# Seven block products for xn^T kn in a fused attention and feed-forward kernel

## Chip, cores and metric

The kernel runs on one core of one Trainium2 chip. The metric is the device time of one execution in microseconds. All data are float32.

## What is computed

The reference takes x of 8 batches by 1024 rows by 256 columns, normalises each row, and adds three things: x itself, a linear attention with 16 heads of 16 columns, and a feed-forward network of width 1024. Cut to what matters:

```python
xn = layernorm(x)
q, k, v = split(xn @ qkv_w + qkv_b)          # 16 heads of 16 columns each
q, k = l2norm(q), l2norm(k)
kv = einsum('bhnd,bhne->bhde', k, v)          # no softmax
attn = einsum('bhnd,bhde->bhne', q, kv) @ proj_w + proj_b
ffn = relu(xn @ W1 + b1) @ W2 + b2
out = x + attn + ffn
```

Since there is no softmax, the kernel does not compute v. It forms G = xn^T kn for each batch (a 256 by 256 matrix, summed over the 1024 rows; kn is the normalised k), then kv from G and the weights of v, and then M = kv proj_w, so that attention ends as one more product, q M, in the accumulation of the second feed-forward product.

## The kernel before, in words

Work goes batch by batch. A batch has 8 row tiles of 128 rows (NT is 8, HT is 4 tiles, a half of the rows); the 256 columns are KC, 2, halves of 128. The order of all instructions is written out by hand: each engine executes its own in the order in which the code issues them, and the framework adds the waits. Tiles come from pools by tag, and most tags ("turn", "u1", "u3", "gT", "xn", "x") have one buffer, so the next tile of a tag waits until all readers of the last one are done.

The loop over b at L822 to L858 has these stages:

- `hidden(b)` (L543) computes the first feed-forward product of batch b. It is already done by Strassen's scheme: a product of 2 by 2 blocks is formed from seven block products of sums of blocks instead of eight. Between its steps stand small steps: `mix_kv` and `mix_m` for M, the scaling and turning of q, and sums of blocks on GpSimd (`sums_of_h`, `sums_of_x`, `sums_of_q`; `sums_of_a` at L188 has the four subtractions and additions at L190, L191, L192 and L194).
- `project_by_sums(b + 1)` (L382) computes q and k of the next batch, by seven products too. It ends with the norms of k: reductions (L377), a maximum, a square root on ScalarE and a reciprocal on VectorE (L352 to L354), while GpSimd adds a bias (L442) and scales k by its norms, half by half (L466).
- `second(b)` (L683) is the second feed-forward product with q M joined to it, by seven products: banks a, c, d and e, of ten matmul records each. After four of them it yields. On VectorE stand u2 and u3 (L702), then, from `between`, `norms_of_q(b + 1)` (four squares on ScalarE at L376, four reductions at L377, L352 to L354), then the joining of bank e (L719) and a 32 by 32 transpose (L710), after which GpSimd adds to x (L715).
- Then come the layer norm statistics of batch b + 2 (`norm_stats` and `norm_scale`: eight statistics at L247, eight aggregations at L249, a root on ScalarE at L251, two small operations at L257 and L260).
- Then `mix_g(b + 1)` (L497): G as 16 matmuls, for each half of the columns of xn eight row tiles, 128 by 128 stationary with 256 columns of kn moving (L502), into one PSUM bank, and one copy to gT on ScalarE (L507).
- Then `norm_apply` (L271) and `turn_x` (L297) of batch b + 2, and the rest of `second(b)`: three more products, their joins, the stores. `shift(b + 2)` ends the round.

An fp32 matmul stands in the profile as two records, each with a weight load of its own, so the 16 matmuls of G are 32 records. The code around the change is this:

Of the kernel before, what the change touches and what calls it, by code (L numbers as in the profile page):

```python
# [9 lines left out]
F32 = mybir.dt.float32  # L10
AF = mybir.ActivationFunctionType
ALU = mybir.AluOpType
# [4 lines left out]
def kernel(  # L17
# [34 lines left out]
    nc = tc.nc  # L52
    P = 128
    B, N, C = x.shape
# [3 lines left out]
    NT = N // P  # L58
    HT = NT // 2
    HN = N // 2  # L60
    KC = C // P
# [11 lines left out]
    one = ctx.enter_context(tc.tile_pool(name="one", bufs=1))  # L73
# [3 lines left out]
    ps_mix = ctx.enter_context(tc.tile_pool(name="ps_mix", bufs=1, space=bass.MemoryType.PSUM))  # L77
# [12 lines left out]
    def bank(shape, name):  # L90

        return psum.tile(shape, F32, tag="bank", name=name)

    xs, xqs, xns, xnTs, xSs, hTs, qks, qTs, mixes, Ms, hSs = ({} for _ in range(11))
# [13 lines left out]
    def load_squares(b, halves=(0, 1)):  # L108
        xqs[b] = one.tile([P, 2, R, HT, CJ], F32, tag="xq", name=f"xq_{b}")
        for n in halves:  # L110
            for j in range(R):
                nc.sync.dma_start(out=xqs[b][ts(j, S), n], in_=squares_v(x, b, n, j))
# [75 lines left out]
    def sums_of_a(eng, blocks, s1, s2, s4, s3=True):  # L188
        a11, a12, a21, a22 = blocks
        eng.tensor_tensor(s1, a21, a22, ALU.add)  # L190
        eng.tensor_tensor(s2, s1, a11, ALU.subtract)  # L191
        eng.tensor_tensor(s4, a12, s2, ALU.subtract)  # L192
        if s3:
            eng.tensor_tensor(a21, a11, a21, ALU.subtract)  # L194
# [46 lines left out]
    def norm_stats(b, tiles):  # L241

        xt, n = xs[b], len(tiles)
        st = work.tile([P, NT, 6], F32, tag="st", name=f"st_{b}_{tiles[0]}")[:, :n, :]
        mv = small.tile([P, NT, 2], F32, tag="mv", name=f"mv_{b}_{tiles[0]}")[:, :n, :]
        for i, t in enumerate(tiles):
            nc.vector.bn_stats(st[:, i, :], xt[:, t, :])  # L247
        for i in range(n):
            nc.vector.bn_aggr(mv[:, i, :], st[:, i, :])  # L249
        rstd = small.tile([P, NT], F32, tag="rstd", name=f"rstd_{b}_{tiles[0]}")[:, :n]  # L250
        nc.scalar.activation(rstd, mv[:, :, 1], AF.Sqrt, bias=eps_sb)  # L251
        for i, t in enumerate(tiles):
            stats[b, t] = i, mv, rstd

    def norm_scale(b, tiles, on_act):
        i, mv, rstd = stats[b, tiles[0]]
        nc.vector.reciprocal(rstd, rstd)  # L257
        if on_act:
            nmr = small.tile([P, NT], F32, tag="nmr", name=f"nmr_{b}_{i}")[:, : len(tiles)]
            nc.vector.scalar_tensor_tensor(nmr, mv[:, :, 0], -1.0, rstd, ALU.mult, ALU.mult)  # L260
            for t in tiles:
                stats[b, t] += (nmr,)
# [87 lines left out]
    def invert(ss):  # L350

        nc.vector.tensor_scalar_max(ss, ss, L2_EPS * L2_EPS)  # L352
        nc.scalar.activation(ss, ss, AF.Sqrt)
        nc.vector.reciprocal(ss, ss)  # L354
# [19 lines left out]
    def squares_of(b, n, g, m, ss):  # L374
        sq = work.tile([P, 2, C], F32, tag="yt", name=f"sq_{b}_{n}_{g}_{m}")
        nc.scalar.activation(sq, part_of_qk(b, n, g, m), AF.Square)  # L376
        return lambda: nc.vector.tensor_reduce(  # L377
            ss[:, n * HT + 2 * g : n * HT + 2 * g + 2, :],
            sq.rearrange("p w (g d) -> p w g d", d=D), AX.X, ALU.add,
        )  # L380
# [69 lines left out]
    def norms_of_q(b):  # L450
        ss = small.tile([P, NT, H], F32, tag="ssq", name=f"ssq_{b}", bufs=1)
        late = []
        for n in range(2):
            for g in range(2):
                late.append(squares_of(b, n, g, 0, ss))
                if len(late) == 2:
                    late.pop(0)()
        late.pop(0)()
        invert(ss)
        for h in range(2):  # L460
            norms_of[b, h, 0] = ss[:, ts(h, HT), :]
# [35 lines left out]
    def mix_g(b):  # L497
        qk, xn = qks[b], xns[b]
        gp = ps_mix.tile([P, KC, C], F32, tag="mix", name=f"gp_{b}")
        for f in range(KC):  # L500
            for t in range(NT):
                nc.tensor.matmul(  # L502
                    gp[:, f, :], xn[:, t, ts(f, P)], qk[:, t, C : 2 * C],
                    start=(t == 0), stop=(t == NT - 1),
                )
        gT = one.tile([P, KC, C], F32, tag="gT", name=f"gT_{b}")
        nc.scalar.copy(gT, gp)  # L507
        mixes[b] = gT

    def mix_kv(b):  # L510
        gT = mixes.pop(b)
        kvp = ps_mix.tile([P, KC, P], F32, tag="mix", name=f"kvp_{b}")
        for c in range(KC):
            cols = slice(2 * C + c * P, 2 * C + (c + 1) * P)
            for f in range(KC):
                nc.tensor.matmul(  # L516
                    kvp[:, c, :], wqkv_sb[:, f, cols], gT[:, f, ts(c, P)],
                    start=(f == 0), stop=(f == KC - 1),
                )
        kvm = one.tile([P, KC, P], F32, tag="Mt", name=f"kvm_{b}")  # L520
        for c in range(KC):
            nc.vector.tensor_tensor(
                kvm[:, c, :].rearrange("p (g d) -> p g d", d=D),
                kvp[:, c, :].rearrange("p (g d) -> p g d", d=D),
                blk.unsqueeze(2).to_broadcast([P, G, D]), ALU.mult,
            )
        mixes[b] = kvm
# [141 lines left out]
    def sums_of_q(b):  # L669
        sums_of_a(  # L670
            nc.vector if b == B - 1 else nc.gpsimd,
            halves(qTs[b]), *(hSs[b][:, s, FH] for s in range(3)),
        )

    def product(dst, lhs, rhs, start, stop):

        for n, (l, r) in enumerate(zip(lhs, rhs)):
            nc.tensor.matmul(  # L678
                dst, l, r, start=start and n == 0, stop=stop and n == len(lhs) - 1,
                skip_group_check=True,  # L680
            )

    def second(b, between=lambda: None):  # L683

        xq, hT, hS, qT, (M, Mt) = xqs[b], hTs[b], hSs[b], qTs[b], Ms[b]
        a11, a12, s3, a22 = (
            [hT[:, i + k * FH, ts(n, HP), :, :] for i in range(FH)] + [qT[:, k, ts(n, HP), :, :]]
            for n in range(2) for k in range(2)
        )
        s1, s2, s4 = ([hS[:, s, i] for i in range(FH + 1)] for s in range(3))  # L690
        b11, t3, b21, b22 = (
            [w2_sb[:, i + k * FH, ts(m, HC)] for i in range(FH)] + [M[:, k, ts(m, HC)]]
            for k in range(2) for m in range(2)
        )
        t1, t2, t4 = ([w2t[:, s, i, :] for i in range(FH)] + [Mt[:, s, :]] for s in range(3))

        def tmp(name):
            pool = work if name in ("u2", "yt") else one
            return pool.tile([P, HP, P, 2], F32, tag=name, name=f"{name}_o_{b}")

        def add(dst, p, q):
            nc.vector.tensor_tensor(dst, p, q, ALU.add)  # L702
            return dst
# [37 lines left out]
        a, c_, d, e = (bank([P, HP, P, 2], f"po{s}_{b}") for s in "acde")  # L741
# [4 lines left out]
        u1 = tmp("u1")  # L746
        nc.scalar.copy(u1, a)
        product(c_, t2, s2, True, True)
        u2 = add(tmp("u2"), c_, u1)
        u3 = tmp("u3")  # L750
        for du, u in zip(ds, parts):
            product(du, t3, [r[:, u] for r in s3], True, False)
# [69 lines left out]
    for b in range(B):  # L822
        if b > 0:
            load_squares(b, (0,) if b == B - 1 else (0, 1))
            if b + 2 < B:
                load(b + 2)
        hidden(b)
        if b == 0:
            qTs[0] = one.tile([P, KC, NP, P, 2], F32, tag="qT", name="qT_0")
            turn_on_pe(qTs[0], qks[0], "q_0")  # L830
            sums_of_w2()
            sums_of_q(0)
            shift(1)
        if b + 1 == 1:
            project(1)
            out_parts = second(b)
        elif b + 1 < B:
            project_by_sums(b + 1)
            out_parts = second(b, lambda: norms_of_q(b + 1))
        else:  # L840
            out_parts = second(b)
        next(out_parts)
        if b + 1 == 1:
            sums_of_x(1, 0)
            sums_of_x(1, 1)
            sums_of_wqk()
        if b + 2 < B:
            norm_stats(b + 2, range(NT))
            norm_scale(b + 2, range(NT), True)
        if b + 1 < B:  # L850
            mix_g(b + 1)
        if b + 2 < B:
            norm_apply(b + 2, range(NT))
            for _ in range(R):
                turn_x(b + 2)
        next(out_parts)
        if b + 2 < B:
            shift(b + 2)  # L858
# [31 lines left out]
```

## Time and profile before

| what | value |
|---|---|
| median of 3 runs | 625.96 us (624.41 to 626.52) |
| the profiled execution's own time | 624.22 us |
| its span, first to last instruction | 622.1 us |
| mean granted TensorE clock | 0.997 |
| VectorE busy | 398.8 us (64%) |
| ScalarE busy | 209.0 us (34%) |
| GpSimd busy | 351.1 us (56%) |
| G, L502: busy in all 8 batches | 56.6 us |
| G: records, mean of one | 256, 379 ns |

The time of an execution is the span and some 2 us around it. The mean of one matmul record includes its way through the array, which overlaps the next one; the pace is read from the start of one group to the start of the next. "Idle before" tells how long an engine had nothing to do before an instruction, and what ended that.

### The profile page before, as it was taken

Reading aid. Unit: us, or ns where it says so; the run is one execution under the profiler, and the core shown is the slowest. Engines: PE = TensorE matmul, PEld = TensorE weight load, DVE = VectorE, ACT = ScalarE, POOL = GpSimd, SP = SyncE. Lnnn points to the kernel's source line nnn. Section 1 sums busy time; section 2 is a strip of 40 time slices with the busy share of each in tenths; the row PEclk is TensorE's granted clock in tenths of the full one; section 3 lists DMA queues with packets and bytes.
Section 4 is the critical chain, followed back from the end, with each engine's and each line's share of the span. In section 5 each row is a group of like instructions: output and inputs, shape, how many; then the busy total and the mean of one; then the engine's idle time right before and its main releaser. Section 6 shows DMA issues by size and latency. Waiting matters only on the chain.

```text
span 622.1 us, 6098 instructions
## 1 busy us (share of the span) xinstructions
PE 612.8 (98%) x1843; PEld 344.2 (55%) x1843; DVE 398.8 (64%) x698; ACT 209.0 (34%) x348; POOL 351.1 (56%) x290
## 2 busy tenths in 40 slices
PE   8999999999999999999999999999999999999996
PEld 5465455556644666447564484644755557545454
DVE  6776735777648766577456874667845677428823
ACT  4356304352143422343242532325224352003500
POOL 3568927399315991269902797029951399414701
PEclk9999999999999999999999999999999999999998
DMA  7734001490025700285004820058101470004202
GB/s 232 141 59 136 1 0 29 112 188 11 0 51 127 161 1 1 68 156 116 0 1 101 189 49 0 6 129 178 29 0 26 112 132 2 0 3 99 67 0 67
DMA packets 139503, 43.26 MB, mean 70 GB/s; under 512 B 135880, under 2 KB 136272, under 8 KB 139472
## 3 DMA queue, kind: packets, MB, share of 16 engines
q1 hardware_dynamic: 139472, 42.89, 31.1%
q8 instruction: 14, 0.23, 0.2%
q14 instruction: 17, 0.14, 0.1%
HBM read 19.80 MB, written 8.39 MB: 45 GB/s over the span
## 4 chain that ended last, share of the span: by engine, by line
PE 96%; DVE 2%; DMA 1%; ACT 0%; issue 0%; SPq 0%; DVEq 0%; ACTq 0%
PE poe L678 11%; PE poa L678 11%; PE pod L678 10%; PE gp L502 9%; PE pha L555 8%; PE phe L555 8%; PE phd L555 8%; PE poc L678 6%; PE pq L330 5%; PE phc L555 4%; PE pqe L398 3%; PE pqa L398 3%; PE pqd L398 3%; PE pqc L398 2%; PE kvp L516 1%; PE mp L533 1%
## 5 line engine op out<-in xcount | busy, mean ns | idle before, releaser
L715 POOL TENSOR_TENSOR xq<-xq,yt_o 128x512 f32<-128x512 f32 x30 | 37.9, 1262 | 181.4 <-DVE yt_o L710 181.4
L562 ACT ACTIVATE hT<-hT,b_sb 128x512 f32<-128x512 f32 x96 | 68.8, 722 | 63.4 <-DVE hT L567 58.8
L190 POOL TENSOR_TENSOR hS<-hT 128x512 f32<-128x512 f32 x31 | 45.8, 1478 | 56.4 <-issue 41.5
L376 ACT ACTIVATE sq<-qk 128x512 f32<-128x512 f32 x48 | 29.0, 629 | 109.3 <-DVE qk L404 59.1
L555 PE MATMUL pha<-xnT,w_sb 128*128 128x512 f32 x128 | 65.4, 592 | 0.0
L678 PE MATMUL poa<-hT,w_sb 128*128 128x512 f32 x128 | 57.5, 592 | 0.0
L502 PE MATMUL gp<-qk,xn 128*128 128x256 f32 x256 | 56.6, 379 | 0.0
L502 PEld LDWEIGHTS gp<-qk,xn 128*128 128x128 f32 x256 | 48.6, 190 | 9.6 <-issue 3.3
L567 DVE TENSOR_TENSOR hT<-phe,u 128x512 f32<-128x512 f32 x64 | 43.7, 683 | 6.6 <-PE phe L555 4.9
L710 DVE STREAM_TRANSPOSE yt_o<-y_o 128x512 f32<-128x512 f32 x30 | 33.0, 1099 | 16.2 <-ACT y_o L765 13.9
L192 POOL TENSOR_TENSOR hS<-hT,hS 128x512 f32<-128x512 f32 x31 | 39.5, 1275 | 2.4
L191 POOL TENSOR_TENSOR hS<-hS,hT 128x512 f32<-128x512 f32 x31 | 39.4, 1272 | 2.4
L194 POOL TENSOR_TENSOR hT<-hT 128x512 f32<-128x512 f32 x31 | 40.0, 1290 | 0.0
L678 PEld LDWEIGHTS poa<-hT,w_sb 128*128 128x128 f32 x128 | 24.3, 190 | 25.0 <-issue 24.2
L297 DVE STREAM_TRANSPOSE turn_x<-xn 128x512 f32<-128x512 f32 x28 | 17.7, 685 | 31.1 <-ACT xn L271 31.1
L555 PEld LDWEIGHTS pha<-xnT,w_sb 128*128 128x128 f32 x128 | 23.8, 190 | 23.4 <-issue 20.8
L567 DVE TENSOR_TENSOR u<-phc,u 128x512 f32<-128x512 f32 x32 | 21.8, 681 | 20.0 <-ACT u L581 10.6
L581 ACT COPY u<-pha 128x512 f32<-128x512 f32 x32 | 18.4, 574 | 43.9 <-PE pha L555 43.9
L562 ACT ACTIVATE hT<-pha,b_sb 128x512 f32<-128x512 f32 x32 | 21.8, 682 | 33.1 <-PE pha L555 33.1
L555 PE MATMUL phe<-xS,w1t 128*128 128x512 f32 x64 | 32.7, 592 | 0.0
L555 PE MATMUL phd<-xnT,w_sb 128*128 128x512 f32 x64 | 32.7, 592 | 0.0
L555 PE MATMUL phc<-xS,w1t 128*128 128x512 f32 x64 | 32.7, 592 | 0.0
(165 smaller groups left out, 1189.6 us busy)
## 6 DMA issues: line engine op xcount, KB each, us to landing
xq<-in_L_attn_x_dram SPq DMA_DIRECT2D x60, 128.0 KB, 3.8
out_dram<-xq SPq DMA_DIRECT2D x60, 128.0 KB, 2.9
x<-in_L_attn_x_dram SPq DMA_DIRECT2D x14, 512.0 KB, 5.8
xnT<-turn_x SPq DMA_DIRECT2D x112, 64.0 KB, 2.1
qT<-turn_q SPq DMA_DIRECT2D x112, 64.0 KB, 2.2
x<-in_L_attn_x_dram SPq DMA_DIRECT2D x4, 256.0 KB, 4.0
w_sb<-in_L_ffn_W_dram SPq DMA_DIRECT2D x2, 512.0 KB, 7.0
w_sb<-in_L_ffn_W_dram SPq DMA_DIRECT2D x8, 128.0 KB, 3.1
```

The lines of the kernel that those rows point to most:

```text
L190: eng.tensor_tensor(s1, a21, a22, ALU.add)
L191: eng.tensor_tensor(s2, s1, a11, ALU.subtract)
L192: eng.tensor_tensor(s4, a12, s2, ALU.subtract)
L194: eng.tensor_tensor(a21, a11, a21, ALU.subtract)
L398: nc.tensor.matmul(dst[:, w, :], a[:, g, :, w], rhs, start=start and w == 0, stop=stop, skip_group_check=True,)
L502: nc.tensor.matmul(gp[:, f, :], xn[:, t, ts(f, P)], qk[:, t, C : 2 * C], start=(t == 0), stop=(t == NT - 1),)
L555: nc.tensor.matmul(dst, lhsT, rhs, start=start, stop=stop, skip_group_check=True)
L562: nc.scalar.activation(block(i, n, m), src, AF.Relu, bias=b1_sb[:, fc : fc + 1])
L567: nc.vector.tensor_tensor(dst, p, q, ALU.add)
L678: nc.tensor.matmul(dst, l, r, start=start and n == 0, stop=stop and n == len(lhs) - 1, skip_group_check=True,)
L710: nc.vector.transpose(yt.rearrange("p u w r c -> p u r w c"), y.rearrange("p u (s r) w -> p u r w s", r=R),)
L715: nc.gpsimd.tensor_tensor(xh, xh, yt.rearrange("p u w r c -> p (u w) r c"), ALU.add)
```

## The change

Batch 0 keeps `mix_g`. For batches 1 to 7 the new `mix_g_by_sums` forms G from blocks: a11, a12, a21, a22 are the blocks of xn (column half by row half), b11 to b22 those of kn (row half by column half). Seven block products of four row tiles each are made, 28 matmuls of 128 moving columns. Bank a is in the pool that mix_g used, banks c, d and e come from the general pool. The products a, d and e are accumulated twice: what stands in the bank after the first product is read by ScalarE (a) or VectorE (d, e) before the second is added. Partial sums us are in a tile of tag "u3".

The sums of blocks of xn are made on VectorE (four operations of 128 by 512, three into a tile of tag "turn", one in place) right after `project_by_sums` or `project`. The sums of blocks of kn are made on GpSimd: three after the scaling of k, a fourth in `between`; they lie in the "turn" tile and in tiles of tags "gT" and "u1". The statistics of batch b + 2 move from behind the first half of `second(b)` to `early`, between u2 and u3. `mix_g` writes gT by one ScalarE copy; the new function by one ScalarE copy and three VectorE additions of 128 by 128.

```diff
+    def g_sums_of_xn(b):
+        gs = one.tile([P, 4, HT, P], F32, tag="turn", name=f"gs_{b}")
+        gsums[b] = [gs[:, i] for i in range(4)]
+        sums_of_a(nc.vector, blocks_of_xn(b), *gsums[b][:3])
+
+    def g_sums_of_kn(b, part):
+        b11, b12, b21, b22 = blocks_of_kn(b)
+        if part == 0:
+            t1 = gsums[b][3]
+            t2 = one.tile([P, HT, P], F32, tag="gT", name=f"gt2_{b}")
+            for dst, p, q in ((t1, b12, b11), (t2, b22, t1), (b12, b22, b12)):
+                nc.gpsimd.tensor_tensor(dst, p, q, ALU.subtract)
+            gsums[b].append(t2)
+        else:
+            t4 = one.tile([P, HT, P], F32, tag="u1", name=f"gt4_{b}")
+            nc.gpsimd.tensor_tensor(t4, b21, gsums[b][4], ALU.subtract)
+            gsums[b].append(t4)
+
+    def mix_g_by_sums(b):
+        a11, a12, s3, a22 = blocks_of_xn(b)
+        b11, t3, b21, b22 = blocks_of_kn(b)
+        s1, s2, s4, t1, t2, t4 = gsums.pop(b)
+        a = ps_mix.tile([P, P], F32, tag="mix", name=f"gpa_{b}")
+        c_, d, e = (bank([P, P], f"gp{s}_{b}") for s in "cde")
+        us = one.tile([P, 3, P], F32, tag="u3", name=f"u_g_{b}")
...
+        mm(a, a11, b11, True, False)
+        nc.scalar.copy(us[:, 0], a)
+        mm(e, s1, t1, True, False)
+        mm(c_, s2, t2, True, True)
+        add(us[:, 1], c_, us[:, 0])
+        mm(d, s3, t3, True, False)
+        add(us[:, 2], d, us[:, 1])
+        gT = one.tile([P, KC, C], F32, tag="gT", name=f"gT_{b}")
+        add(gT[:, 1, P:C], e, us[:, 2])
+        mm(a, a12, b21, False, True)
+        nc.scalar.copy(gT[:, 0, 0:P], a)
+        mm(d, a22, t4, False, True)
+        add(gT[:, 1, 0:P], d, us[:, 1])
+        mm(e, s4, b22, False, True)
+        add(gT[:, 0, P:C], e, us[:, 1])
+        mixes[b] = gT
...
@@ second
         u2 = add(tmp("u2"), c_, u1)
+        early()
         u3 = tmp("u3")
...
@@ the loop over b
-            out_parts = second(b, lambda: norms_of_q(b + 1))
+        if b + 1 < B:
+            g_sums_of_xn(b + 1)
+            g_sums_of_kn(b + 1, 0)
+
+            def early():
+                if b + 2 < B:
+                    norm_stats(b + 2, range(NT))
+                    norm_scale(b + 2, range(NT), True)
+
+            def between():
+                g_sums_of_kn(b + 1, 1)
+                if b > 0:
+                    norms_of_q(b + 1)
+
+            out_parts = second(b, early, between)
...
-        if b + 2 < B:
-            norm_stats(b + 2, range(NT))
-            norm_scale(b + 2, range(NT), True)
         if b + 1 < B:
-            mix_g(b + 1)
+            mix_g_by_sums(b + 1)
```

More of the change, by code (lines that the diff above doesn't have):

```diff
@@ L508, in mix_g, with blocks_of_xn, blocks_of_kn @@
         mixes[b] = gT
+    gsums = {}
+    def blocks_of_xn(b):
+        return [xns[b][:, ts(n, HT), ts(f, P)] for f in range(KC) for n in range(2)]
+    def blocks_of_kn(b):
+        return [
+            qks[b][:, ts(n, HT), C + f * P : C + (f + 1) * P] for n in range(2) for f in range(KC)
+        ]
+    def g_sums_of_xn(b):
+        gs = one.tile([P, 4, HT, P], F32, tag="turn", name=f"gs_{b}")
+        gsums[b] = [gs[:, i] for i in range(4)]
+        sums_of_a(nc.vector, blocks_of_xn(b), *gsums[b][:3])
@@ new lines, in mix_g_by_sums, with mm, add @@
+    def mix_g_by_sums(b):
[5 more added lines that the diff above has]
+        us = one.tile([P, 3, P], F32, tag="u3", name=f"u_g_{b}")
+        def mm(dst, l, r, start, stop):
+            for t in range(HT):
+                nc.tensor.matmul(
+                    dst, l[:, t, :], r[:, t, :], start=start and t == 0,
+                    stop=stop and t == HT - 1, skip_group_check=True,
+                )
+        def add(dst, p, q):
+            nc.vector.tensor_tensor(dst, p, q, ALU.add)
+        mm(a, a11, b11, True, False)
[14 more added lines that the diff above has]
+        mixes[b] = gT
@@ L681, in product, with second @@
             )
-    def second(b, between=lambda: None):
+    def second(b, early=lambda: None, between=lambda: None):
         xq, hT, hS, qT, (M, Mt) = xqs[b], hTs[b], hSs[b], qTs[b], Ms[b]
@@ L835 @@
             project(1)
-            out_parts = second(b)
         elif b + 1 < B:
             project_by_sums(b + 1)
-            out_parts = second(b, lambda: norms_of_q(b + 1))
+        if b + 1 < B:
[10 more added lines that the diff above has]
+            out_parts = second(b, early, between)
         else:
```

## The prediction

> **What bounds the kernel now.** I read the page's busy times and its chain first: is one engine the bound, and does it ever wait?
>
> ```profile
> PE 612.8 (98%) x1843; PEld 344.2 (55%) x1843; DVE 398.8 (64%) x698; ACT 209.0 (34%) x348; POOL 351.1 (56%) x290
> PE 96%; DVE 2%; DMA 1%; ACT 0%; issue 0%; SPq 0%; DVEq 0%; ACTq 0%
> ```
>
> TensorE holds 98% of the span and 96% of the chain, and in the table of waits its longest wait is 1.4 us, at the start. So a shorter product on TensorE shortens the kernel by as much, and any wait that is put into TensorE lengthens it by as much. The question is what the new product costs in pace and in waits. Second view, the timeline of TensorE: the same kind of product at several widths (start, duration, group, records).
>
> ```profile
> 113.55 1.05 PE L516 MATMUL kvp<-gT,wqkv_sb 128*128 128x128 f32 x8
> 114.44 1.02 PE L555 MATMUL pha<-xnT,w_sb 128*128 128x512 f32 x2
> ...
> 314.81 7.07 PE L502 MATMUL gp<-qk,xn 128*128 128x256 f32 x32
> 321.72 3.60 PE L678 MATMUL poa<-hT,w_sb 128*128 128x512 f32 x8
> ```
>
> From start to start, 32 records of 256 columns take 6.91 us, 216 ns each; 8 records of 128 columns take 0.89 us, 111 ns each. Third view: what VectorE and GpSimd do around the sums, with the round that makes G of batch 4 as the sample (the other rounds show the same distances within 0.1 us). GpSimd:
>
> ```profile
> 302.55 1.27 POOL L194 TENSOR_TENSOR qT<-qT 128x512 f32<-128x512 f32 x1
> 303.77 2.35 POOL L442 TENSOR_TENSOR qk<-qk,dbias 128x1024 f32<-128x1024 f32 x1
> 306.08 3.83 POOL L466 TENSOR_TENSOR qk<-qk,ssk 128x1024 f32<-128x1024 f32 x2
> ```
>
> and VectorE:
>
> ```profile
> 301.70 0.95 DVE L354 RECIPROCAL ssk<-ssk 128x128 f32<-128x128 f32 x1 [0.38 <-ACT ssk L353]
> 306.50 0.69 DVE L702 TENSOR_TENSOR u_o<-poc,u_o 128x512 f32<-128x512 f32 x1 [3.84 <-PE poc L678]
> 310.72 0.69 DVE L702 TENSOR_TENSOR u_o<-pod,u_o 128x512 f32<-128x512 f32 x1 [3.53 <-PE pod L678]
> ...
> 315.55 0.65 DVE L719 SCALAR_TENSOR_TENSOR y_o<-poe,ob,u_o 128x512 f32<-128x512 f32 x1
> ...
> 317.34 2.67 DVE L247 BATCH_NORM_STATS2 st<-x 128x6 f32<-128x256 f32 x8
> ```
>
> VectorE seems to have room: 3.84 us and 3.53 us of idle time before u2 and u3, just where the sums of xn and the statistics are put. But GpSimd works without a gap until 309.9. Fourth view, one line's forms, and the only place where VectorE makes such sums today, in the last batch:
>
> ```profile
> L352 DVE TENSOR_SCALAR ssk<-ssk x6: 976/988/1098, 150.7 to 524.8; 128x128 f32<-128x128 f32 x6
> L352 DVE TENSOR_SCALAR ssq<-ssq x6: 226/227/228, 164.4 to 538.5; 128x128 f32<-128x128 f32 x6
> ```
>
> ```profile
> 585.68 1.38 DVE L190 TENSOR_TENSOR hS<-hT 128x512 f32<-128x512 f32 x1
> 587.10 1.64 DVE L191 TENSOR_TENSOR hS<-hS,hT 128x512 f32<-128x512 f32 x1
> 588.84 0.69 DVE L192 TENSOR_TENSOR hS<-hT,hS 128x512 f32<-128x512 f32 x1
> ```
>
> ```profile
> 585.24 1.27 POOL L192 TENSOR_TENSOR hS<-hT,hS 128x512 f32<-128x512 f32 x1
> 586.47 1.71 POOL L194 TENSOR_TENSOR hT<-hT 128x512 f32<-128x512 f32 x1
> ```
>
> The same operation takes 0.99 us while GpSimd works (ssk) and 0.23 us when it rests (ssq). The sums show how: L190 is issued at 585.68, does not run until GpSimd's L192 ends at 586.51, and ends at 587.06, 0.55 us later. GpSimd's L194 is issued at 586.47 and ends 1.12 us after VectorE's L190. VectorE's L191 waits for that in turn and ends 0.56 us after it. They alternate, one whole instruction each. Once GpSimd is done, 0.69 us is the full price.
>
> **The change, part by part.**
>
> *The product.* 28 matmuls are 56 records; at 111 ns, 6.23 us for 6.91: minus 0.68 us, 4.8 us over seven batches. Here a rule speaks against the change: the Trainium skill, TensorE: Matmul & The Clock Gate, Back-to-back issue gap, has the weight loads set part of the spacing, about 81 ns sustained for 128 bf16 columns where the columns alone give 56. An estimate from that page's 25 ns excess on each record is 136 ns, 7.6 us for 56: a loss of 0.7 us a batch. The row says 111 ns (and the 16 transposes of 128 columns in batch 0 start 109 ns apart, a load each); I take 111.
>
> *The sums of xn on VectorE*, four operations, no DMA. Alone they would take 2.6 us (4 by 0.65) and lie in the 3.84 us gap, at nothing. But VectorE is free at 302.65, 0.1 us after GpSimd began L194. By the alternation: first sum ends 303.82 + 0.55 = 304.4; the bias, 2.35 less the 0.15 that L194 had overlapped, ends at 306.6; second sum 307.1; first scaling 308.9; third sum 309.5; second scaling 311.3; fourth sum 311.8. That is 9.2 us, not 2.6. (Fourth directly after third, on which it doesn't depend: 310.0.) Behind it wait u2, everything in VectorE's queue, and ScalarE's queue through it.
>
> *The sums of kn on GpSimd.* Each 1.27 us: done at 312.9, 314.3, 315.5, the fourth at 316.8. The products need them at 315.7, 316.6, 317.5 and 319.3: hidden by GpSimd's former idle time (309.9 to 317.5), 0.8 us or more to spare each; without that cover each us would be paid in full.
>
> *The statistics, moved ahead.* They cost VectorE the same 3.98 us (317.34 to 321.32) and have no DMA. They leave the place behind the transpose, where nobody on TensorE waited, and stand now before u3, the four reductions, L352 to L354, the joining of bank e and the transpose. ScalarE's root L251 now stands ahead of the four squares, so the squares, before done two by two from 302.62 on, wait for it too. u2 311.8 to 312.4; statistics to 316.4, and L260, which reads two tensors, waits for GpSimd's fourth sum: 316.95. So u3 starts at 316.95, not 310.72: 6.2 us late. The first two squares end by 317.4, before u3 does, so they add nothing.
>
> *The new waits.* The rest of VectorE's queue follows 6.2 us late: bank e joined 321.8 to 322.4, transpose to 323.5, then the additions of G, 0.28 us each (nearest row: kvm, 128 by 128 from PSUM, L522), first 323.5, second ending 324.2. TensorE: first products of a, e, c, d 314.81 to 318.4. The second product of a needs ScalarE's copy of us, which waits for u3 to be read (same tag), by the joining at 322.4: copy 0.3 us (nearest: L353, 0.31), so a starts at 322.9. d needs the second addition: 324.3; e is ready. End 324.3 + 1.78 = 326.1 instead of 321.72. Behind TensorE's wait is queued all the rest of `second(b)`. **Plus 4.35 us** in each of the five rounds that have all these parts (G of batches 2 to 6).
>
> *The two other rounds.* G of batch 7 has no statistics: u3 only 1.6 us late, d starts at 319.75 instead of 319.27; minus 0.68 plus 0.48, minus 0.2. G of batch 1: the norms of q aren't there, GpSimd's scaling ends at 80.86, VectorE's sums at about 85.2, u3 by 90.6, when bank e is done (90.5) as before; no wait, minus 0.68.
>
> *The clock.* In five rounds TensorE now rests about 4.5 us (318.4 to 322.9). Before, it never does within the span; only the end shows what rest does:
>
> ```profile
> 618.00:619.00 1.00, 0.00 (x0) 0.00 (x0) 0.00 (x0) 0.00 (x0) 0.00 (x0) 0.94 0.76 175
> 619.00:620.00 1.00, 0.00 (x0) 0.00 (x0) 0.00 (x0) 0.00 (x0) 0.00 (x0) 0.50 0.99 372
> ```
>
> (stretch, length, busy time of five engines, then the granted clock). The last matmul ended at 616.66; the clock halved near 618.9, 2.2 us later. The same page, Part 1, asks for an idle window of some 3.4 us that runs freely: by it alone about (4.5 - 3.4)/3.4, 3 in 10, of such rests would halve the clock; by this row, where such a window would hold 0.85 us of work, nearly 6 in 10. A drop lasts under 4 us (the 20 warm-up transposes took 3.90 us, 195 ns each, against 109), so it costs at most 2 us, less the 0.5 us for which d waits anyway: 1.5. Bounds 0 and 7.5 us for five rounds; I take two, 3.0.
>
> *Sum.* 624.2 + 5 x 4.35 - 0.2 - 0.7 + 3.0 = **648** us. This stands on the profiled execution, 1.7 us below the median shown; either is well inside what follows.
>
> **The rivals.**
>
> 1. *The fourth sum follows the third at once.* VectorE is done at 310.0, u3 at 315.6, a at 321.6, d at 323.0: plus 3.1 us in five rounds, minus 0.7 in two: 638, 639 or 640 with a drop. For it: the last two sums don't depend on each other. Against: GpSimd's L192 and L194 were back to back too, and VectorE came between.
> 2. *No wait: faster.* If the sums keep to their 0.69 us (say VectorE gets ahead of GpSimd each time), they end at 305.4, u2 stays at 306.5, statistics end at 311.1, u3 is 0.4 us late, the second addition ends at 318.9, before d can start. Then seven times minus 0.68: 619.5. The point is u3's delay: up to 1.1 us nothing is lost, above it TensorE pays one for one. Against it stand L352 and L190, each in every place where both engines meet.
> 3. *Narrow products are slow.* At 136 ns a record the products lose 0.7 us instead of gaining it, in the first part, second and all: another 5 to 10 us on top, 653 to 658. Against: both rows at 109 to 111 ns, though of 8 and 16 records only.
> 4. *In between:* a wait of 1 to 2.5 us, 622 to 635, if GpSimd's order leaves VectorE a gap that I don't see.
>
> **How the numbers follow.** My forecast 0.47 (645 without a drop of the clock, 653 with all), rival 1 0.23, rival 2 0.11, rival 3 0.08, rival 4 0.11. About 0.3% (1.9 us) is what a measurement of this kernel can tell from no change. Rival 2 is all faster; of rival 4 a third is within 0.3%; the rest slower. The range 636 to 657 leaves out rivals 2 and 4 and the top of 3.
>
> **What would show it.** Right: the sums of xn (L190 to L194 on VectorE) with means above 1.3 us, taking about 9 us from first to last; u3 (L770 of the changed kernel) some 6 us later against bank d; TensorE waiting at the second product of a for ScalarE, and at d for VectorE, near 5 us a round in five rounds and under 1 in two; records of G 111 ns apart; the granted clock below 1 in some slices. Wrong: sums at 0.69 us, or TensorE's waits under 1 us in all rounds, or a pace of G's records near 136 ns.

## The result, and the profile after

The changed kernel takes 644.62 us (median of 6 runs, 644.03 to 646.48) where the kernel before takes 624.51 us (6 runs): a ratio of 1.0322, 95% interval 1.030 to 1.0343. It is 20.1 us slower. The profiled execution has a span of 642.4 us, 20.3 us more, and a mean granted clock of 0.981.

First view, the page: busy times, the clock in 40 slices, the chain.

```profile
PE 619.6 (96%) x2011; PEld 355.3 (55%) x2011; DVE 462.5 (72%) x761; ACT 210.1 (33%) x355; POOL 399.4 (62%) x318
...
PEclk9999999999899998999989999799998999999998
...
PE 74%; DVE 20%; issue 2%; ACT 2%; DMA 0%; DVEq 0%; ACTq 0%
```

TensorE was 96% of the chain and is 74%; VectorE, formerly 2%, holds 20%. The clock row, full before except at its end, has a dent in each of five rounds. Second view, the waits of TensorE (who waited for whom, us in total, times, longest):

```profile
PE gpa L553 <- ACT u_g L562: 14.3, 5, 2.9
...
PE gpd L553 <- DVE u_g L559: 0.4, 1, 0.4
```

The first line is new and stands in five rounds: the second product of bank a waits for ScalarE's copy of its first. Third view, TensorE's timeline while it makes G of batch 4, and of batch 7, the round without early statistics:

```profile
322.03 1.05 PE L553 MATMUL gpa<-qk,xn 128*128 128x128 f32 x8
...
324.71 1.06 PE L553 MATMUL gpd<-qk,xn 128*128 128x128 f32 x8
328.64 2.08 PE L553 MATMUL gpa<-qk,xn 128*128 128x128 f32 x8 [2.87 <-ACT u_g L562]
330.51 1.57 PE L553 MATMUL gpd<-gt,xn 128*128 128x128 f32 x8
331.92 1.06 PE L553 MATMUL gpe<-qk,gs 128*128 128x128 f32 x8
332.81 3.60 PE L746 MATMUL poa<-hT,w_sb 128*128 128x512 f32 x8
```

```profile
560.27 1.05 PE L553 MATMUL gpa<-qk,xn 128*128 128x128 f32 x8
...
566.52 3.60 PE L746 MATMUL poa<-hT,w_sb 128*128 128x512 f32 x8
```

Without a wait G takes 6.25 us (112 ns a record) instead of 6.90: the seven products do what they should. With it, batch 4 takes 10.78 us. From the starts, batches 2 to 6 take 11.04, 10.94, 10.78, 11.88 and 11.37 us, 21.5 us more than five times 6.90; in batch 5 the product behind is 0.45 us long too. Less 2 x 0.65 us in the other two rounds, this is 20.7 us, and the span grew by 20.3. The 0.4 us between the two is not accounted for; but for that, the loss is in these five places.

Fourth view, VectorE ahead of and during G of batch 4, then GpSimd and one line of ScalarE at the same time:

```profile
309.83 0.63 DVE L190 TENSOR_TENSOR gs<-xn 128x512 f32<-128x512 f32 x1
310.49 1.63 DVE L191 TENSOR_TENSOR gs<-gs,xn 128x512 f32<-128x512 f32 x1
312.16 2.72 DVE L192 TENSOR_TENSOR gs<-xn,gs 128x512 f32<-128x512 f32 x1
314.80 2.42 DVE L194 TENSOR_TENSOR xn<-xn 128x512 f32<-128x512 f32 x1
...
321.58 1.26 DVE L260 SCALAR_TENSOR_TENSOR nmr<-mv,rstd 128x8 f32<-128x8 f32 x1
322.77 0.68 DVE L770 TENSOR_TENSOR u_o<-pod,u_o 128x512 f32<-128x512 f32 x1
...
327.58 0.65 DVE L787 SCALAR_TENSOR_TENSOR y_o<-poe,ob,u_o 128x512 f32<-128x512 f32 x1
```

```profile
309.81 1.77 POOL L194 TENSOR_TENSOR qT<-qT 128x512 f32<-128x512 f32 x1
311.54 2.79 POOL L442 TENSOR_TENSOR qk<-qk,dbias 128x1024 f32<-128x1024 f32 x1
314.29 4.71 POOL L466 TENSOR_TENSOR qk<-qk,ssk 128x1024 f32<-128x1024 f32 x2
```

```profile
328.32 0.27 ACT L562 COPY u_g<-gpa 128x128 f32<-128x128 f32 x1 [1.64 <-DVE y_o L787]
```

Both engines are held up, and each by the other. GpSimd's L194 takes 1.77 us instead of 1.27, 0.5 us more, while the first sum runs; VectorE's L191 ends 0.54 us after that L194 (at 311.58); GpSimd's L442 takes 2.79 instead of 2.35; VectorE's L192 ends 0.55 us after it. A sum that is worth 0.69 us takes up to 2.72. The four take 7.4 us, and u3 (L770 on bank d) starts 0.74 us after G begins, where before it started 4.09 us ahead of it: 4.8 us late. L787, which reads u3 and so frees the tile that ScalarE's copy writes to, ends at 328.2, and the copy at 328.6: that is when TensorE resumes. The small L260, 0.17 us before, takes 1.26 us, behind a sum of GpSimd.

### The profile page after: what moved, and what is told of

The parts are those of the page before. It is cut to its first block, busy times and chain, and to the rows that moved or that the text cites. A ratio compares the mean times of both kernels' runs of the same rounds, so it can differ in the third digit from the quotient of the medians.

```text
span 642.4 us, 6595 instructions
## 1 busy us (share of the span) xinstructions
PE 619.6 (96%) x2011; PEld 355.3 (55%) x2011; DVE 462.5 (72%) x761; ACT 210.1 (33%) x355; POOL 399.4 (62%) x318
## 4 chain that ended last, share of the span: by engine, by line
PE 74%; DVE 20%; issue 2%; ACT 2%; DMA 0%; DVEq 0%; ACTq 0%
PE pha L623 8%; PE phe L623 8%; PE phd L623 8%; PE poa L746 7%; PE poe L746 7%; PE pod L746 7%; PE pq L330 4%; PE phc L623 4%; DVE qk L404 3%; DVE st L247 2%; PE poc L746 2%; PE pqd L398 2%; PE pqe L398 2%; PE pqa L398 2%; DVE xn L194 2%
## 5 line engine op out<-in xcount | busy, mean ns | idle before, releaser
L190 POOL TENSOR_TENSOR hS<-hT 128x512 f32<-128x512 f32 x31 | 46.5, 1499 | 55.7 <-ACT hT L630 55.7
L192 POOL TENSOR_TENSOR hS<-hT,hS 128x512 f32<-128x512 f32 x31 | 39.5, 1276 | 2.4
L191 POOL TENSOR_TENSOR hS<-hS,hT 128x512 f32<-128x512 f32 x31 | 39.5, 1274 | 2.4
L194 POOL TENSOR_TENSOR hT<-hT 128x512 f32<-128x512 f32 x31 | 39.9, 1289 | 0.0
L623 PE MATMUL phe<-xS,w_sb 128*128 128x512 f32 x64 | 32.7, 592 | 0.0
L623 PE MATMUL phd<-xnT,w1t 128*128 128x512 f32 x64 | 32.7, 592 | 0.0
L553 PE MATMUL gpa<-qk,xn 128*128 128x128 f32 x112 | 18.6, 320 | 14.3 <-ACT u_g L562 14.3
```

The lines of the kernel that those rows point to most:

```text
L623: nc.tensor.matmul(dst, lhsT, rhs, start=start, stop=stop, skip_group_check=True)
```

## The experiments

Theory 1: VectorE's sums of xn take turns with GpSimd; together with the statistics they make VectorE's queue so late that TensorE waits inside G, and this rest of TensorE halves its clock. Rivals: the moved statistics alone do it; the sums alone do it; the slow records after the wait have another cause than the clock. The first four are compared with 624.13 us for the kernel before, the last two with 624.57 us, runs on the same chip each.

**Without the sums of xn.** Plain blocks take their places, so this kernel leaves out a part of the computation and its G is another matrix.

```diff
-        sums_of_a(nc.vector, blocks_of_xn(b), *gsums[b][:3])
+        a11, a12, a21, a22 = blocks_of_xn(b)
+        gsums[b] = [a21, a11, a12, gs[:, 3]]
```

> The changed kernel without the four VectorE operations that make the sums of blocks of xn; plain blocks of xn take their places in the products, so G is not the reference's. TensorE, GpSimd and the early statistics are as in the changed kernel. Theory 1 (the sums wait in turn with GpSimd and make VectorE's queue late): u3 is about 0.4 us late, no wait at the second product of a, clock full, 7 x 0.65 us gained: 620 us, and GpSimd's bias and scaling are back at 2.35 and 1.93 us. Rival (the statistics moved ahead, with their root ahead of the squares, make it late by themselves): TensorE still waits 2 us or more in five rounds, 634 us or more.

Measured: 619.97 us, ratio 0.9925 (0.9899 to 0.995). TensorE's waits at G are gone. VectorE and GpSimd ahead of G of batch 4:

```profile
305.68 0.69 DVE L770 TENSOR_TENSOR u_o<-poc,u_o 128x512 f32<-128x512 f32 x1 [3.82 <-PE poc L746]
...
310.26 0.68 DVE L770 TENSOR_TENSOR u_o<-pod,u_o 128x512 f32<-128x512 f32 x1
```

```profile
302.96 2.35 POOL L442 TENSOR_TENSOR qk<-qk,dbias 128x1024 f32<-128x1024 f32 x1
```

VectorE has its 3.82 us of idle time back, and GpSimd's bias and scaling have their old length (2.35 and, for both halves, 3.82 us): it was VectorE's sums that slowed GpSimd. The other direction shows at the end of the changed kernel, where VectorE makes sums of the same size with GpSimd at rest (from 610.39 on): four of them take 0.68 or 0.69 us each. The early statistics fit between u2 and u3, which starts 3.73 us ahead of G (313.99), 0.36 us late. The rival that the moved statistics alone do harm is out.

**Statistics behind the products of G.** The sums stay on VectorE.

```diff
-            def early():
...
         if b + 1 < B:
             mix_g_by_sums(b + 1)
         if b + 2 < B:
+            norm_stats(b + 2, range(NT))
+            norm_scale(b + 2, range(NT), True)
             norm_apply(b + 2, range(NT))
```

> The changed kernel with the statistics of batch b + 2 issued after the products of G instead of between u2 and u3; the sums of xn stay on VectorE. Theory 1 with slack: the sums alone end about 4.8 us before G starts, u3 is 0.5 us late, under the 1.1 us that cost nothing, so no wait inside G; the late statistics push the scaling of xn and the turning by about 3 us, which may cost TensorE a few tenths at the start of the next hidden: 621 to 624 us. Rival (the sums alone suffice for the wait): 632 us or more with waits at the second product of a.

Measured: 619.4 us, ratio 0.9917 (0.9891 to 0.9943). In the timeline of VectorE the sums are as slow as in the changed kernel, and nothing waits for them:

```profile
302.93 2.72 DVE L192 TENSOR_TENSOR gs<-xn,gs 128x512 f32<-128x512 f32 x1
...
308.69 0.69 DVE L770 TENSOR_TENSOR u_o<-pod,u_o 128x512 f32<-128x512 f32 x1
```

G starts at 312.65 and the next product at 318.90. So u3 starts 3.96 us ahead of G, 0.13 us late, and G takes its 6.25 us. The contention is all there and costs nothing; the feared tenths at the next hidden didn't come either. So it takes both, the slowed sums and the statistics, to go past the slack.

**The sums of xn on GpSimd**, in turn with those of kn:

```diff
-        sums_of_a(nc.vector, blocks_of_xn(b), *gsums[b][:3])
...
+            for dst, p, q, op in (
+                (s1, a21, a22, ALU.add), (t1, b12, b11, ALU.subtract),
+                (s2, s1, a11, ALU.subtract), (t2, b22, t1, ALU.subtract),
+                (a21, a11, a21, ALU.subtract), (b12, b22, b12, ALU.subtract),
+            ):
+                nc.gpsimd.tensor_tensor(dst, p, q, op)
...
             nc.gpsimd.tensor_tensor(t4, b21, gsums[b][4], ALU.subtract)
+            nc.gpsimd.tensor_tensor(s4, a12, s2, ALU.subtract)
```

> The changed kernel with the four sums of xn on GpSimd, behind the scaling of k and in turn with the sums of kn; VectorE has none of them. Theory 1: VectorE is on time (u3 0.4 us late), GpSimd has the last sum of kn 4.1 us and the last of xn 5.4 us after G starts, just when d and e want them: waits under 0.3 us a round, 620 to 622 us. Rival (GpSimd, 62 percent busy, becomes the bound): the second products of d and e wait for it by more than 1 us a round, 630 us or more.

Measured: 619.28 us, ratio 0.992 (0.9893 to 0.9947), no wait at G. The lines of GpSimd's last sums (this kernel has its own line numbers):

```profile
315.07 1.29 POOL L544 TENSOR_TENSOR gt<-qk,gt 128x512 f32<-128x512 f32 x1
316.30 1.27 POOL L546 TENSOR_TENSOR gs<-xn,gs 128x512 f32<-128x512 f32 x1
```

GpSimd ends its last sum of kn 3.7 us after the start of G (312.67) and its last of xn 4.9 us after it, ahead of the 4.46 and 5.36 us at which TensorE asks for them. On GpSimd, one after another, the four sums of xn take 5.1 us (1.26 to 1.29 each); on VectorE, which needs 0.69 us for one when it is alone, they took 7.4 us beside a busy GpSimd.

**The clock held up.** Twelve matmuls that nobody reads are put in front of the second product of a, in the five rounds with a wait:

```diff
...
+        if 2 <= b < B - 1:
+            for t in range(12):
+                nc.tensor.matmul(
+                    free[b][:, 0, :, 0], ident, ident, start=True, stop=True, skip_group_check=True
+                )
         mm(a, a12, b21, False, True)
...
         u2 = add(tmp("u2"), c_, u1)
+        free[b + 1] = c_
```

> The changed kernel with 12 matmuls of 128 columns more (24 records, 2.7 us, into a bank that nobody reads any more) ahead of the second product of a, in the five rounds in which TensorE waits there. All else is the same, the wait for ScalarE too. Theory (the long rest halves the clock, and the records after it run at about half pace): the clock stays at 1.0, the records after the wait are 111 ns apart, and with some 1.6 us a round gained the time is 636 to 638 us. Rival (the slow records after the wait are the price of the wait itself, say of the weight loads starting anew): no change, 644 to 645 us.

Measured: 637.85 us, ratio 1.0211 (1.0188 to 1.0234), 6.8 us less than the changed kernel (6.4 if each is counted from the kernel before of its own comparison), though TensorE does more work. First the stretches of the wait and behind it in the changed kernel (length, busy times of TensorE, its weight loads, VectorE, ScalarE and GpSimd, granted clock, DMA share and GB/s), then the stretch with the twelve matmuls and TensorE's timeline here:

```profile
325.70:328.60 2.90, 0.07 (x1) 0.00 (x0) 2.39 (x5) 0.57 (x2) 0.00 (x0) 0.93 0.00 0
328.60:330.50 1.90, 1.86 (x8) 1.86 (x9) 1.61 (x4) 0.00 (x0) 0.96 (x1) 0.50 0.00 0
```

```profile
324.20:327.00 2.80, 2.64 (x23) 2.45 (x23) 2.32 (x4) 0.57 (x2) 0.00 (x0) 1.00 0.00 0
```

```profile
323.59 2.84 PE L572 MATMUL poc<-ident 128*128 128x128 f32 x24
326.59 1.16 PE L553 MATMUL gpa<-qk,xn 128*128 128x128 f32 x8 [0.16 <-ACT u_g L562]
...
329.08 1.06 PE L553 MATMUL gpe<-qk,gs 128*128 128x128 f32 x8
```

The clock stays full and the records after the wait take their normal pace; the wait is still there, filled for the most part with the twelve matmuls. G takes 9.95 us here (320.02 to 329.97): 3.7 us of wait a round above 6.25, and in the changed kernel another 6.8 / 5, 1.4 us, through the clock. The traces agree: the five rounds of the changed kernel lie 25.2 us above 6.25 each (with the 0.45 us behind batch 5), of which five waits of 3.7 us leave 6.7.

**Half of the statistics early.**

```diff
...
-                    norm_stats(b + 2, range(NT))
-                    norm_scale(b + 2, range(NT), True)
+                    norm_stats(b + 2, range(HT))
+                    norm_scale(b + 2, range(HT), True)
...
             mix_g_by_sums(b + 1)
+        if b + 2 < B:
+            norm_stats(b + 2, range(HT, NT))
+            norm_scale(b + 2, range(HT, NT), True)
```

> The changed kernel with the statistics of only four of the eight row tiles between u2 and u3; the other four stand behind the products of G. Theory (above a slack of about 1.1 us TensorE pays for u3's delay one for one): u3 is 2.4 us late instead of 4.8, the second product of a waits 0.6 us and that of d another 0.6 us, too short a rest for the clock to fall, so 5 x 1.2 us above the versions without a wait: 625 to 626 us, up to 628 if the small operation on two tensors is held up by GpSimd again. Rival (the clock falls after any rest of some tenths): 631 us or more. Rival (what matters is the number of operations ahead of u3 and not their sum): as the full move, above 640 us.

Measured: 626.78 us, ratio 1.0035 (1.0023 to 1.0047).

```profile
PE gpa L553 <- ACT u_g L562: 3.2, 5, 0.6
PE gpd L553 <- DVE u_g L559: 1.8, 5, 0.4
```

```profile
313.90 0.68 DVE L770 TENSOR_TENSOR u_o<-pod,u_o 128x512 f32<-128x512 f32 x1
...
317.25 0.62 DVE L352 TENSOR_SCALAR ssq<-ssq 128x128 f32<-128x128 f32 x1
```

In batch 4 u3 is 2.2 us late (313.90, with G at 315.79), G takes 7.76 us, 1.5 more than without a wait, 0.3 more than expected; five times 1.5 above 619.3 is 626.8. The clock is 1.0 throughout the profiled execution. So the delay counts by its size, less a slack: 0.7 us here (2.2 less 1.5), 1.1 us in the changed kernel (4.8 less 3.7). Most of that difference is the small L352 behind u3, which takes 0.62 us here and 0.23 us there, where it comes so late that GpSimd has nothing more to do. A rest of 0.6 us leaves the clock alone.

**TensorE's order changed alone.** The product of bank a, which needs nothing of G, goes between the first four and the last three block products of G:

```diff
         add(gT[:, 1, P:C], e, us[:, 2])
+        yield
         mm(a, a12, b21, False, True)
...
         turn_back(0, 0, y)
+        yield
         product(e, b22, s4, False, True)
...
         if b + 1 < B:
-            mix_g_by_sums(b + 1)
+            g_parts = mix_g_by_sums(b + 1)
+            next(g_parts)
+        next(out_parts)
+        if b + 1 < B:
+            next(g_parts)
```

> The changed kernel with TensorE's order changed alone: the product of bank a in the second half of the second feed-forward product (4.3 us, it needs nothing of G) stands between the first four and the last three block products of G. VectorE's sums, its statistics and their delays stay. Theory: TensorE has work while ScalarE and VectorE read the banks, the second product of a starts 7.9 us after G's start and finds its copy done (6.6 us): no wait, clock full, 619 to 621 us, with u3 still 4.8 us late. Rival (a late VectorE costs TensorE elsewhere, at the joins or at the next hidden): 625 us or more.

Measured: 620.24 us, ratio 0.9926 (0.9906 to 0.9945). u3 starts at 315.19, 0.69 us after G (314.50), as late as in the changed kernel, and TensorE doesn't wait:

```profile
315.19 0.68 DVE L772 TENSOR_TENSOR u_o<-pod,u_o 128x512 f32<-128x512 f32 x1
```

```profile
314.50 1.05 PE L553 MATMUL gpa<-qk,xn 128*128 128x128 f32 x8
...
318.07 3.60 PE L748 MATMUL poa<-hT,w_sb 128*128 128x512 f32 x8
...
322.36 1.05 PE L553 MATMUL gpa<-qk,xn 128*128 128x128 f32 x8
```

VectorE being late costs TensorE nothing anywhere else. The versions without the wait stand at 619.3 to 620.2 us. Leaving aside the one that leaves the sums out, none of them is clearly ahead. Each is 0.7 to 0.8% faster than the kernel before, with the whole interval below 1, and so faster than the changed kernel too.

## Why the prediction was right

The forecast was 648 us, 636 to 657, slower with 0.85; measured 644.6. The path to the loss was the forecast one: sums held up by GpSimd, VectorE late, TensorE waiting inside G, its clock falling. That the number lies so near is in part luck, since two terms were off in opposite directions. By its steps:

- *The product*: minus 0.68 us a round was forecast, minus 0.65 measured. The 136 ns estimated for narrow records is 112 measured, so rival 3 is out.
- *The sums of xn*: the mechanism was right, whole instructions in turn, and the size too large: 9.2 us forecast, 7.4 measured. I took VectorE to come 0.1 us too late for a turn ahead of GpSimd's L194; in the trace it is issued 0.02 us after it and goes first all the same. So each later sum waited for one GpSimd instruction earlier than forecast: the second for L194, the third for the bias, the fourth for the first half of the scaling (2.42 us). The fourth did not follow the third at once, so rival 1's reason is out, though its length for the four sums, 310.0 less 302.65 or 7.4 us, is the measured one. So u3 was 4.8 us late, not 6.2, and the waits are 3.7 us a round, not 5.0.
- *The sums of kn*: hidden, as forecast. *L260* held up by GpSimd: as forecast, 1.26 us.
- *The new waits*: a for ScalarE's copy behind the joining of bank e, in five rounds, as forecast. The wait of d for VectorE's second addition was to come in the same five; in the changed kernel it shows in one (0.35 us, batch 6), since the slowed second product of a covers it in the others, and with the clock held up it is there in all five (0.36 us). In batch 7, plus 0.5 us was forecast and no wait came.
- *The clock*: two drops in five were taken, 3.0 us in all; it fell in all five rounds and cost 6.8 us. This is the term that was too small, and it hid much of the term that was too large: 5 x 5.0 + 3.0 is 28 us forecast and 5 x 3.7 + 6.8, 25 us, measured. The forecast gave 645 us without a drop and 653 with all five; all five came, and 644.6 lies just below both. With the clock held up the kernel takes 637.85 us, which is rival 1's 638. The estimated chances of a drop, 3 or 6 in 10, were both too low for what was five in five, although the rests were shorter (2.9 us) than the 4.5 us they were made for.
- *The signs*: the means of three of the four sums are above 1.3 us (1.73, 2.56 and 2.32); L190's, 0.69, is not, since it went ahead of GpSimd in six of seven rounds (0.63 us, and 1.05 in the seventh).
- Rival 2, no wait, is what all the versions at 619 to 620 us show: its 619.5 was right for a kernel whose VectorE isn't late, or is late where it doesn't count.

## What to carry to other kernels

Idle time of an engine is room only for work whose operands don't bring it against a busy neighbour: cost VectorE's operations on two SBUF tensors at their own length and that of the GpSimd instruction that they can meet. Two moves that each fit into the same slack must be added before either is called free. When a product is split so that its partial sums are read in between, put independent TensorE work into that gap; a wait of 2.9 us there was paid twice, once as time and once as clock, and one of 0.6 us once.

## What the runs showed of the hardware

- A rest of 2.9 us was enough to halve TensorE's clock in five of five rounds; a rest of 0.6 us never did. In batch 4 it fell some 2.4 us after the last matmul: that ended at 325.77, and a mean of 0.93 over the 2.90 us to 328.60 makes about 0.4 us at half clock. In batch 2 it fell only after work had begun again (clock 1.00 up to 170.70, mean 0.58 in the 2.8 us from there, work again from 170.78), and in batch 6 too (1.00 up to 488.50, work again from 487.58).
- The clock stayed low longer than the under 4 us that I took from the start of the kernel: in batch 5 from about 406.7 to 413.5 (means of 0.89, 0.50, 0.50 and 0.87 over 404.4 to 407.3, to 410, to 413 and to 415), 6.9 us, the last 6.2 of them with TensorE at work.
- Operations of 128 by 8 elements wait in the same way as large ones: L260 takes 1.26 us for 0.17 where GpSimd is busy.
